# Two convolutions as four diagonal products each, and the second layer's set-up inside the mixers' plan

## The chip, the cores and the metric

The kernel runs on one core of a Trainium2 chip. The core has five engines that run side by side and wait for one another by semaphores: PE (TensorE, matrix products into PSUM), DVE (VectorE), ACT (ScalarE), POOL (GpSimd) and SP (SyncE, which here only issues DMA transfers). The metric is the device time of one execution in microseconds; before the change it is 6781.04 us, the median of three runs (6777.89 to 6788.52).

## The reference, cut to what matters

The input x has 4 images of 256 channels and 64x64 places, so 4 sequences of 4096 tokens. Two layers follow each other, and after them a mixture of experts. Everything is float32.

```python
# layer 0: a Mamba mixer with 512 inner channels and 16 states
xm, zm = split(t @ m_in_w.T)                       # 512 channels each
xp = pad(xm, 3 zeros in front of each sequence)
xc = sum(xp[:, k:k+L] * m_conv_w[:, k] for k in range(4)) + m_conv_b
xm = silu(xc)                                      # then dt, B, C from xm; a scan over the tokens:
h = exp(dt*A) * h + (dt*xm) * B ; y = (h * C).sum(states)

# layer 1: rmsnorm, one projection W_in, the same kind of convolution over 4 tokens on 512 + 128 channels
z, xBC, dt = split(rmsnorm(t, norm_w) @ W_in.T)
xBC = silu(sum(pad(xBC)[:, k:k+L] * conv_w[:, k] for k in range(4)) + conv_b)
# ... a scan with 8 heads, rmsnorm with gnorm_w, W_out; then 8 experts, each token to the best one (gate_w)
```

Each convolution multiplies a channel's last four tokens by that channel's own four weights ("taps") and adds them; no channel mixes with another.

## The kernel before

The program has three phases: `mixers` (both layers and the routing), `experts` and `turn` (back to channels first). The change is in `mixers` alone and in the host's layout of two weight arrays.

**Tiling.** Tokens are cut into 64 chunks of T = 256 (16 per sequence). A tile has 128 channels as partitions, and tokens or groups beside them. For each chunk the stages are `front0` (projection and convolution of layer 0), `mid0` (step sizes), `scan` (16 steps; each makes `ub` and `h` on DVE over 128x1024 elements, and `p` on POOL), `tail0` (output projection), `front1` (layer 1's norm, projection and convolution), `ssd` (layer 1's scan in matrix form, two chunks later) and `back1` (routing).

**Order of the work.** Before the chunks a set-up part is written out in program order (lines 442 to 614): it loads the weights, folds norm weights into them and makes small helper matrices. Loads of layer 0's weights are issued by SP, those of layer 1's by ACT's queue. After it, everything is recorded by `Plan` (line 136) rather than issued: each operation has a slot, which is its chunk's number times 16 plus the stage's own (FRONT0 = -25, MID0 = -16, scan 0 to 15, TAIL = 18, SSD = 29, BACK = 37). `Plan.order` (line 273) then places the operations by estimated durations: whenever an engine is free, it takes the ready operation with the lowest slot. The estimates are constants in `mm`, `act`, `dve`, `gps` and `dma`. The resulting order is fixed at build time; on the chip each engine runs its list in that order and waits where an input is late. Every operation of the plan has line 371 in the profile, where it is issued, so tile names tell them apart.

**Buffers.** A tile is named by a tag with a number of buffers. `raw` (the convolution's input with three tokens of the chunk before in front, the "halo") has one buffer, which both layers use in turn; `raw4` has three. In PSUM the banks are `a` (two buffers, `front0` and `mid0`), `b` (one, `tail0` and `front1`), `c` (two, `ssd` and `back1`), `ub` (one) and `py` (one). A new tile in a tag begins when the last reader of the old one is done. The halo is written by POOL (`halo`, line 661), and the last three tokens are kept by POOL for the next chunk (`keep`, line 668).

**The convolution.** `to_taps` (line 677) writes `raw` to a DRAM buffer `raw_d`. For each of the four groups j of 128 channels `tapped` (line 683) reads it back with four DMAs into `raw4`: 32 partitions per tap, each shifted by one token, four channel groups beside one another. `convolve` (line 693) makes four products with 128x32 weights, each of which fills 32 of PSUM's partitions:

```python
for i in range(SQ):
    r.mm(pi[i * R : (i + 1) * R], weights[:, j * SQ + i], raw4[:, i], start=True, stop=True)
r.act(dst, pi, AF.Identity, bias=bias[:, j : j + 1])
```

The weights `taps_m` and `taps_x` hold 16 such 128x32 matrices each. A float32 product is recorded as two matmul instructions. The remaining 128 channels of layer 1 (B and C) are convolved in another way already: `diag_bc` holds four diagonal 128x128 matrices, and `front1` (lines 1018 and 1019) adds four products over the shifted tile `rbc`.

## Time and profile before

| what | value |
|---|---|
| median of three runs | 6781.04 us |
| the profiled execution | 6786.87 us |
| its span, first to last instruction | 6785.2 us |
| PE, DVE, ACT, POOL busy | 5984.4, 5545.7, 4859.2, 3494.2 us |
| first matmul of the plan (`a<-xin,w_cen`) | 43.58 us |
| first `ub` of a scan | 110.50 us |
| `xin` loads of chunks 7 and 58 issued at | 484.68 and 4823.53 us |
| DMA moved | 1245.58 MB |
| of it `raw<-raw_d`, 2048 transfers of 128.0 KB | 3.8 us each to landing (median) |
| `raw_d<-raw`, 128 transfers of 518.0 KB | 4.2 us each to landing (median) |

"Busy" is the time in which an engine has an instruction of its own in hand; matmuls are pipelined, so PE's busy time includes the ends of products that overlap nothing. "PEclk" is the share of full clock that TensorE was granted. In lines with `<-` the tile written stands on the left and those read on the right; a number after "idle before" is the time that the engine waited, and the arrow names what ended the wait. SPq and ACTq are the queues of SP and ACT that issue DMAs. The median lies 5.8 us under the profiled execution and 4.2 us under its span.

### The profile page before, as it was taken

To read this page: it belongs to the slowest core of one execution; us is meant where nothing else is said; L and a number is where in the kernel's file an instruction comes from. 1 tells how busy PE (TensorE), PEld (TensorE's weight loads), DVE (VectorE), ACT (ScalarE), POOL (GpSimd) and SP (SyncE) were. 2 spreads that over 40 slices of the span, in tenths; PEclk is the share of its full clock that TensorE was granted. 3 is DMA by queue.
4 is the path that set the end of the run, shared out by engine and by line. 5 is a ranking of instruction groups with operands and counts; after the bars stand their busy time and mean duration, and the time that the engine had idled before them with its cause. 6 is when DMAs were issued, how large, how long until landed. Compare 5 with 4: busy or idle time off the path is not lost. (4 is left out here: it accounts for less than half of the span.)

```text
span 6785.2 us, 114276 instructions
## 1 busy us (share of the span) xinstructions
PE 5984.4 (88%) x37672; PEld 4045.8 (60%) x37672; DVE 5545.7 (82%) x7646; ACT 4859.2 (72%) x12007; POOL 3494.2 (51%) x2632
## 2 busy tenths in 40 slices
PE   5788888888888888888888888888888877999996
PEld 3455555555555555555555555555555546888885
DVE  3889999999999999999999999999999973344333
ACT  4778888888888888888888888888888852333332
POOL 3555555555555555555555555555555552333331
PEclk7889999999999999999999999999999988999998
DMA  6976777777777777777777777777777734555556
GB/s 177 254 184 179 183 181 181 181 184 184 181 181 177 180 181 183 184 182 182 183 182 183 183 183 181 184 183 183 183 183 181 178 102 152 193 193 191 187 194 243
DMA packets 1125138, 1245.58 MB, mean 184 GB/s; under 512 B 111888, under 2 KB 1093652, under 8 KB 1115330
## 3 DMA queue, kind: packets, MB, share of 16 engines
q1 hardware_dynamic: 1083458, 1008.76, 59.1%
q0 software_dynamic: 30000, 210.98, 8.8%
q10 hardware_dynamic: 11088, 18.53, 0.7%
q8 instruction: 300, 4.92, 0.3%
q14 instruction: 292, 2.39, 0.1%
HBM read 919.92 MB, written 311.63 MB: 182 GB/s over the span
## 5 line engine op out<-in xcount | busy, mean ns | idle before, releaser
L371 POOL TENSOR_TENSOR p<-h,bc 128x1024 f32<-128x1024 f32 x1024 | 2413.3, 2357 | 1995.3 <-DVE ub L371 578.3
L371 DVE TENSOR_TENSOR_SCAN h<-da,ub 128x1024 f32<-128x1024 f32 x1024 | 2338.9, 2284 | 80.4 <-ACT da L371 4.8
L371 ACT ACTIVATE da<-dt,w_m_Alog 128x255 f32<-128x255 f32 x4096 | 1830.7, 502 | 0.5 <-issue 0.5
L371 DVE TENSOR_TENSOR ub<-u,bc 128x1024 f32<-128x1024 f32 x1024 | 1269.1, 1239 | 20.2 <-DMA u<-u_d 11.3
L371 PE MATMUL py<-p,sum 128*32 128x256 f32 x8192 | 689.6, 411 | 334.1 <-POOL p L371 326.3
L371 PE MATMUL b<-t,w_W_in 128*128 128x256 f32 x2304 | 581.5, 393 | 65.1 <-ACT raw L371 26.1
L371 PEld LDWEIGHTS py<-p,sum 128*32 128x32 f32 x8192 | 180.7, 111 | 724.6 <-POOL p L371 465.2
L371 PEld LDWEIGHTS b<-t,w_W_in 128*128 128x128 f32 x2304 | 420.8, 191 | 230.6 <-ACT raw L371 90.3
L1374 PE MATMUL ph<-xt,w 128*128 128x256 f32 x2272 | 517.8, 381 | 5.2 <-ACT hid L1376 5.0
L1385 PE MATMUL po<-w,hid 128*128 128x256 f32 x2272 | 502.0, 379 | 0.0
L371 PE MATMUL a<-t,w_m_in_w 128*128 128x256 f32 x2048 | 496.6, 391 | 4.5 <-DVE t L371 4.5
L371 ACT COPY hlast<-h 128x4 f32<-128x4 f32 x1024 | 202.6, 198 | 407.3 <-DVE h L371 402.8
L1385 PEld LDWEIGHTS po<-w,hid 128*128 128x128 f32 x2272 | 431.7, 190 | 58.7
L1374 PEld LDWEIGHTS ph<-xt,w 128*128 128x128 f32 x2272 | 427.4, 191 | 64.8 <-ACT hid L1376 7.6
L371 PEld LDWEIGHTS a<-t,w_m_in_w 128*128 128x128 f32 x2048 | 377.0, 191 | 125.8 <-issue 50.6
L1351 DVE CAST number<-rows 128x2 uint32<-128x2 f32 x71 | 12.2, 172 | 486.0 <-DMA tok_d<-fixed,number 473.6
L371 PE MATMUL c<-cum,after 128*128 128x512 f32 x512 | 331.2, 752 | 83.8 <-ACT dend L371 67.3
L1349 ACT ACTIVATE tn<-rows 128x256 f32<-128x256 f32 x142 | 82.2, 597 | 421.0 <-DMA rows<-buf_d,row_at 420.6
L1397 POOL DMA_INDIRECT tok_d<-fixed,number x142 | 145.8, 1027 | 396.3 <-DVE fixed L1395 306.1
L371 ACT ACT_TABLE_LOAD x256 | 328.4, 1283 | 4.4
L371 ACT ACTIVATE cum<-upto,da 128x128 f32<-128x128 f32 x1024 | 328.7, 395 | 0.7 <-DVE da L371 0.7
L1376 ACT ACTIVATE hid<-ph,w 128x256 f32<-128x256 f32 x426 | 187.4, 468 | 143.7 <-PE ph L1374 143.1
(237 smaller groups left out, 11289.3 us busy)
## 6 DMA issues: line engine op xcount, KB each, us to landing
raw<-raw_d SPq DMA_DIRECT2D x2048, 128.0 KB, 3.8
dt<-dt_d SPq DMA_DIRECT2D x1024, 128.0 KB, 3.2
u<-u_d SPq DMA_DIRECT2D x1024, 128.0 KB, 3.9
raw_d<-raw SPq DMA_DIRECT2D x128, 518.0 KB, 4.2
gx_d<-pre SPq DMA_DIRECT2D x64, 1024.0 KB, 4.5
bc<-bc_d SPq DMA_DIRECT2D x1024, 64.0 KB, 2.4
gx<-gx_d SPq DMA_DIRECT2D x256, 256.0 KB, 5.2
dt_d<-mid SPq DMA_DIRECT2D x64, 512.0 KB, 2.9
```

The source lines that it names most:

```text
L371: op.issued = f(*map(placed, args), **{k: placed(v) for k, v in kw.items()})
L1349: act(tn[:, j], rows[:, j, TOK:], AF.Identity, scale=rows[:, j, 1:2], bias=rows[:, j, 2:3])
L1351: nc.vector.tensor_copy(number, rows[:, :, 3])
L1374: mm(ph, w1[:, k, f * P : (f + 1) * P], xt[:, k], start=k == 0, stop=k == KC - 1)
L1376: act(hid[:, f], ph, AF.Relu, bias=b1[:, f : f + 1])
L1385: mm(po[:, j], hid[:, f, j * P : (j + 1) * P], w2[:, f], start=f == 0, stop=f == KF - 1)
L1397: nc.gpsimd.indirect_dma_start(out=tok_d, out_offset=bass.IndirectOffsetOnAxis(ap=number[:, j : j + 1], axis=0), in_=fixed[:, j], in_offse ...
```

## The change

Both convolutions read `raw` in SBUF directly. The weights become 16 diagonal 128x128 matrices for each layer (four channel groups by four taps), and each group is four accumulating products of 128x128 by 256. `to_taps`, `tapped`, `raw_d` and `raw4` are gone. The host lays the tap weights out by channel. The loads and the weight arithmetic of layer 1 leave the set-up and are recorded in the plan with slots from -22 to 0, all loads on SP. The loads of layer 0 come in another order, and `neg_a0` is computed later. TAIL is 19 instead of 18, and the plan's estimate for DVE operations of at most four elements is 0.1 us more than their elements instead of 0.14. `lasting` stops the plan's list of former readers from growing for the constants; it changes no instruction by itself.

```diff
-TAIL, SSD, BACK = 18, 29, 37
+TAIL, SSD, BACK = 19, 29, 37
...
-        op = self.note("DVE", (0.06 if n > 4 else 0.14) + n / 960, ...
+        op = self.note("DVE", (0.06 if n > 4 else 0.1) + n / 960, ...
...
         w_in = load("w_in")
         w_gate = load("w_gate")
+        m_in = load("m_in_w")
+        ln_b = load("ln_b")
+        m_cw = load("m_conv_w")
+        ln_g = load("ln_g")
         b_gate = load("b_gate")
-        ln_g = load("ln_g")
-        ln_b = load("ln_b")
-        m_in = load("m_in_w")
-        m_cw = load("m_conv_w")
...
-        act(neg_a0, neg_a0, AF.Exp)
-        ts(neg_a0, neg_a0, -1.0, None, ALU.mult)
-        s_in = wp.tile([P, KC, 2 * DI + 2 * N2 + NH + NE], F32, name="w_W_in", tag="w_W_in")
-        nc.scalar.dma_start(s_in[:, :, :-NE], a["W_in"])
-        s_cw = load("conv_w", nc.scalar)
-        s_cb = load("conv_b", nc.scalar)
...
-        act(neg_a1, neg_a1, AF.Exp)
-        ts(neg_a1, neg_a1, -1.0, None, ALU.mult)
-        for k in range(KC):
-            ts(s_in[:, k, :-NE], s_in[:, k, :-NE], s_nw[:, k : k + 1], None, ALU.mult)
-        for k in range(KD):
-            ts(s_out[:, k, :C], s_out[:, k, :C], s_gn[:, k : k + 1], None, ALU.mult)
...
-        diag_d1 = diagonal(s_d, "diag_d1")
-        diag_bc = diagonal(s_cwbc, "diag_bc")
-        taps_m = taps(m_cw, "taps_m")
-        taps_x = taps(s_cw, "taps_x")
+        taps_m = diagonal(m_cw, "taps_m")
...
-        g_cen = g_w
...
-        nc.scalar.copy(s_in[:, :, -NE:], g_cen)
-        for k in range(KD):
-            pt_s = bank_a()
-            for m in range(KC):
-                nc.tensor.transpose(pt_s[:, m * P : (m + 1) * P], s_out[:, k, m * P : (m + 1) * P], ident)
...
+        act(neg_a0, neg_a0, AF.Exp)
+        ts(neg_a0, neg_a0, -1.0, None, ALU.mult)
         py = py_p.tile([P, 512], F32, name="py0", tag="py", bufs=1)
-        mm(py, ident, s_in[:, 0, :512], start=True, stop=True)
+        mm(py, ident, m_in[:, 0, :512], start=True, stop=True)
...
+        def later(n, name, shape=None):
+            r.slot(n)
+            src = a[name]
+            t = r.fixed(wp.tile(list(shape or src.shape), F32, name=f"w_{name}", tag=f"w_{name}"))
+            r.dma("SP", t if shape is None else t[:, :, : src.shape[-1]], src)
+            return t
+
+        def later_diagonal(n, scales, name):
+            k = scales.shape[1]
+            t = r.fixed(wp.tile([P, k, P], F32, name=name, tag=name))
+            for i in range(k):
+                r.slot(n + 0.2 * i)
+                r.gps("tensor_scalar", t[:, i], ident, scales[:, i : i + 1], None, ALU.mult)
+            return t
+
+        s_in = later(-22, "W_in", [P, KC, 2 * DI + 2 * N2 + NH + NE])
+        s_nw = later(-22, "norm_w")
+        s_out = later(-18, "W_out", [P, KD, C + NE])
+        s_gn = later(-18, "gnorm_w")
+        g_w = later(-18, "gate_w")
+        s_cw = later(-17, "conv_w")
+        s_cwbc = later(-17, "conv_w_bc")
+        s_d = later(-17, "Dp")
+        s_cb, s_cbbc, s_dtb, neg_a1, g_b = (
+            later(-16, n) for n in ("conv_b", "conv_b_bc", "dt_bias", "A_log", "gate_b")
+        )
+        taps_x = later_diagonal(-6, s_cw, "taps_x")
+        diag_bc = later_diagonal(-2, s_cwbc, "diag_bc")
+        diag_d1 = later_diagonal(0, s_d, "diag_d1")
+        r.slot(-8)
+        r.act(neg_a1, neg_a1, AF.Exp)
+        r.dve("tensor_scalar", neg_a1, neg_a1, -1.0, None, ALU.mult)
+        for k in range(KC):
+            r.dve("tensor_scalar", s_in[:, k, :-NE], s_in[:, k, :-NE], s_nw[:, k : k + 1], None, ALU.mult)
+        for k in range(KD):
+            r.dve("tensor_scalar", s_out[:, k, :C], s_out[:, k, :C], s_gn[:, k : k + 1], None, ALU.mult)
+        pt_s = bank_c(NE)
+        for k in range(KC):
+            r.mm(pt_s, mean_c, g_w[:, k], start=k == 0, stop=k == KC - 1)
+        for k in range(KC):
+            r.tt(g_w[:, k], g_w[:, k], pt_s, ALU.subtract)
+        r.copy(s_in[:, :, -NE:], g_w)
+        for k in range(KD):
+            pt_s = bank_c(KC, P)
+            for m in range(KC):
+                r.transpose(pt_s[:, m], s_out[:, k, m * P : (m + 1) * P], ident)
+            turned = work([P, KC, P], "sq")
+            r.copy(turned, pt_s)
+            pt_s = bank_c(NE)
+            for m in range(KC):
+                r.mm(pt_s, turned[:, m], g_w[:, m], start=m == 0, stop=m == KC - 1)
+            r.copy(s_out[:, k, C:], pt_s)
+        for t in (s_in, s_out, s_cb, s_cbbc, s_dtb, neg_a1, g_b, taps_x, diag_bc, diag_d1):
+            t.root.lasting = True
...
-        def to_taps(raw, tag):
-            d = scratch([NG, R, TAPS - 1 + T], tag)
-            r.dma("SP", spread_rows(d), raw)
-            return d
-        def tapped(d, j):
-            t = work([P, SQ, T], "raw4", 3)
-            for k in range(TAPS):
-                r.dma("SP", t[k * R : (k + 1) * R], d[j * SQ : (j + 1) * SQ, :, k : k + T].rearrange("g c l -> c g l"))
-            return t
-        def convolve(raw4, weights, j, dst, bias, get):
+        def convolve(raw, weights, j, dst, bias, get):
             pi = get(T)
-            for i in range(SQ):
-                r.mm(pi[i * R : (i + 1) * R], weights[:, j * SQ + i], raw4[:, i], start=True, stop=True)
+            for k in range(TAPS):
+                r.mm(pi, weights[:, j * TAPS + k], raw[:, j, k : k + T], start=k == 0, stop=k == TAPS - 1)
             r.act(dst, pi, AF.Identity, bias=bias[:, j : j + 1])
...
             for j in range(KD):
                 k_.at(FRONT0 + 5 + j)
-                part = tapped(d, j)
                 k_.at(FRONT0 + 7 + j)
-                convolve(part, taps_m, j, pre0[:, KC + KD + j], m_cb, bank_a)
+                convolve(raw, taps_m, j, pre0[:, KC + KD + j], m_cb, bank_a)
...
-                convolve(part, taps_x, j, pre1[:, KD + j], s_cb, bank_b)
+                convolve(raw, taps_x, j, pre1[:, KD + j], s_cb, bank_b)
...
-        return np.asarray(w).reshape(NG, R, TAPS).transpose(2, 1, 0).reshape(P, NG)
+        return np.asarray(w).reshape(KD, P, TAPS).transpose(1, 0, 2).reshape(P, KD * TAPS)
```

## The prediction

> **What bounds the kernel now.** I read the page's totals and slices first, then busy time by stage, then the waits of DVE and PE in the repeating stretch, then single groups of PE's timeline. The page's totals and slices:
>
> ```profile
> span 6785.2 us, 114276 instructions
> PE 5984.4 (88%) x37672; PEld 4045.8 (60%) x37672; DVE 5545.7 (82%) x7646; ACT 4859.2 (72%) x12007; POOL 3494.2 (51%) x2632
> ...
> PE   5788888888888888888888888888888877999996
> DVE  3889999999999999999999999999999973344333
> PEclk7889999999999999999999999999999988999998
> DMA  6976777777777777777777777777777734555556
> ```
>
> From slice 4 to slice 32 DVE is at 9 tenths and PE just below it; the last fifth (experts, output) is PE's and is not touched. The windows of the filling, the crowded beginning and the repeating stretch (busy us and instructions by engine, granted clock, DMA share, GB/s):
>
> ```profile
> 44.00:110.00 66.00, 40.05 (x152) 27.27 (x150) 6.28 (x6) 25.97 (x47) 0.58 (x3) 0.74 0.49 134
> 110.00:430.00 320.00, 242.28 (x1504) 149.79 (x1504) 276.36 (x303) 237.55 (x585) 162.38 (x110) 0.83 0.93 237
> 430.00:5250.00 4820.00, 4294.03 (x28794) 2714.10 (x28788) 4497.81 (x6002) 3985.25 (x9957) 2756.24 (x1959) 0.94 0.73 182
> ```
>
> The loads of xin of chunks 7 and 58 are 4338.85 us apart: 85.08 us per chunk, so 4820 us hold 56.7 chunks. Per chunk DVE is busy 93.3%, or 79.4 us, and idle 5.7; PE is busy 89.1%, or 75.8 us, and idle 9.3. The waits in that stretch:
>
> ```profile
> DVE xdt L371 <- PE c L371: 77.1, 131, 2.6
> DVE state L371 <- PE c L371: 55.8, 48, 1.2
> DVE gm L371 <- PE c L371: 36.1, 44, 2.6
> PE py L371 <- POOL p L371: 266.1, 204, 4.4
> PE c L371 <- ACT dend L371: 64.6, 53, 1.5
> ```
>
> DVE waits for no DMA here. What it waits for is PE's ssd products, about 3 us per chunk in these three lines. PE's longest wait is for p, the end of a scan step, 4.7 us per chunk: PE runs ahead and waits for DVE's and POOL's chain. So DVE sets the pace, and PE has slack. How much is the whole question, because the change takes from it.
>
> **What the Trainium skill says.** TensorE: Matmul & The Clock Gate, Part 1: the clock has two states, full and half, set by how busy PE was in windows of some 3.4 us. The trace agrees: slices of 10 us show 1.00, and 0.50 between 70 and 80 us; from 5700 to 6300 us, where PE is busy 595.96 of 600, it is 1.00. So the mean of 0.94 means half clock 12% of the time: it costs PE up to 0.06 x 85.08 = 5.1 us per chunk, and a denser PE may win part of it back. TensorEngine Tiling (Array Packing), Overview: weights of 32 columns leave room for four products side by side, up to 4 times faster. The trace shows close to 3, below. Perfetto Trace Analysis, Identifying the Most-Contended Engine: PE's busy share is a poor measure of its headroom; hence I count PE by products at full clock.
>
> **The price of a product.** Groups of PE's timeline (start, us, tiles, records; two records are one product):
>
> ```profile
> 3007.21 0.61 PE L371 MATMUL a<-raw,taps_m 128*32 128x256 f32 x8
> 3015.93 3.62 PE L371 MATMUL b<-g,w_m_out_w 128*128 128x256 f32 x16
> 3024.88 1.89 PE L371 MATMUL a<-pre,w_m_xproj_w 128*64 128x256 f32 x8
> 3059.46 2.00 PE L371 MATMUL b<-rbc,diag_bc 128*128 128x256 f32 x8 [0.84 <-ACT pre L371]
> ```
>
> The last line is the new form already in use, four diagonal products. Alone it is busy 2.00 us; in a backlog the second eight records of 16 cost 3.62 - 1.89 = 1.73. A tap group costs 0.61 to 0.64. A convolution group so grows by 1.1 us (1.73 - 0.64) to 1.4 (2.00 - 0.64), and a chunk has eight: 8.7 to 10.9 us more PE per chunk. I take 8.7, since PE will be backlogged.
>
> **The change part by part.**
>
> *Steady pace.* PE's need at full clock is at most 75.8 - 5.1 = 70.7 us per chunk now, and 70.7 + 8.7 = 79.4 after: as much as DVE. The 85.08 us leave 14.4 us of loss now (9.3 idle, 5.1 half clock). To hold the pace, the losses must fall to 5.7. The 4.7 us of waiting for p are slack and go first; two thirds of the half clock, 3.4 us, go if the pauses that cause it close; 0.6 must come from waits for ACT (dend, raw, bcs), which other products can fill. That just suffices. DVE's own work stays 79.4.
>
> *DMA removed.* Per chunk 2 writes of 518 KB and 32 reads of 128 KB, 34 issues by SP of about 0.45 us: 15 us less of SP's queue and 5.1 MB less. Worth nothing in the steady stretch, because DVE waits for none of it; SP's own waits for free raw4 tiles stood only before transfers that were needed later.
>
> *New holds.* raw has one buffer for both layers. It was free about 4 us after the write to DRAM; now PE's last convolution product frees it. POOL's halo copy waits for that, and POOL's p products queue behind the copy. At 3000 us layer 1 held raw from about 3046 and its convolutions end at 3076.6; layer 0's input products begin at 3066.9, so they must start some 10 us later. Layer 0's convolutions at 3000 to 3014 show that the time is there: about 52 us of 85 are held. Zero, unless POOL stands for more than two scan steps (7.3 us), the three h tiles being the cover. Bank b's single buffer is held 4 x 1.1 us longer per chunk, of some 60 us in use: also zero.
>
> *Set-up.* These are rows of the timeline from the start:
>
> ```profile
> 21.75 0.57 ACT L535 COPY w_nat<-bank_a 128x512 f32<-128x512 f32 x1
> 25.95 6.83 PE L567 MATMUL bank_a<-w_ln_b,w_m_in_w 128*128 128x1 f32 x32
> 43.58 2.64 PE L371 MATMUL a<-xin,w_cen 128*128 128x256 f32 x8
> 66.33 1.08 PE L371 MATMUL a<-raw,taps_m 128*32 128x256 f32 x8 [5.73 <-DMA raw<-raw_d]
> 110.50 1.23 DVE L371 TENSOR_TENSOR ub<-u,bc 128x1024 f32<-128x1024 f32 x1 [10.43 <-DMA u<-u_d]
> ```
>
> The w_nat copy is ready at 4.8 us, but ACT stands issuing layer 1's loads until 21.6. Afterwards: copy at 4.9, the w_gate products (3.78 us) to 9.5; m_in is third among the loads, 1.5 MB at the 191 GB/s of the first 10 us, there at about 9; the 6.83 us of L567 to 16.4; the copy 0.17 and the scaling of m_in 1.45 to 18.2; the warm-up product 2.05 to 20.3. The plan's first matmul moves from 43.6 to 20.3: 23.3 us gained. The 16 diagonals of taps_m cost POOL 16 x 0.75 = 12 us, from about 10 to 22, and are wanted at about 42.
>
> *What is moved into the plan.* 13 loads, 13 x 0.47 = 6 us of SP, which is idle from 10.5 to 48, and 1.7 MB; DVE 3.4 us, ACT about 3, PE about 8 (1.0 + 2.7 + 4.1); POOL 24 diagonals, 18 us. The window 44 to 110 shows DVE busy 6.28 of 66 and POOL 0.58, so all of it fits before layer 1 first needs it. Without that cover it would cost up to those 18 us once. I take zero.
>
> *The first chunk's convolution.* raw was ready at 58.0, the last tap group's evacuation ended at 75.2. Now PE goes on after m_in's second half (60.6): 4 x 1.73 = 6.9 and an evacuation of 0.47, at 68.0: 7 us. So the first ub comes 30 us earlier, near 80.
>
> *The crowded beginning.* From 110 to 430 us DVE is busy 86.4% against 93.3% later, 22 us lost, with DMA at 0.93 of its engines and the clock at 0.83. Tap transfers are about 5 chunks x 5.1 MB = 26 of 76 MB. Bounds are 0 and 22; I take 10.
>
> *Small estimates and TAIL 19.* They only reorder; the same operations run. Bounds of half a us per chunk either way, about 28 us; I take zero.
>
> Sum against the span: -23.3 - 7 - 10 = -40, 6785 to 6745. The median is 4 us under the span: 6781 - 40 = **6741**.
>
> **The rivals.**
>
> *PE becomes the bound (slower).* PE at 79.4 has no room for its waits. For: it would have to lose only 5.7 us per chunk where it loses 14.4; PE would be at work in 93% of the time with DVE also at 93%, each waiting for the other. If only p's 4.7 and half of the clock's loss (2.5) go, 7.2 us remain: 86.6 us per chunk, 1.5 more, 56.7 x 1.5 = 86; with 10.9 in place of 8.7 it is 3.7 more, 210. A backlogged PE is nearer the low end: 1.9 gives 6741 + 108 = **6849**. It decides at 40 / 56.7 = 0.7 us more per chunk: there the start's gain is eaten. Against: the experts' stage shows PE able to run without pauses.
>
> *The pace rises.* With DMA crossings gone, products come when the plan wants them, and PE stays at full clock just when DVE waits for ssd. Half of DVE's three waits for c, 1.5 us per chunk, saves 85: **6656**. Against: more work stands ahead of ssd's products in PE's queue.
>
> *The convolution's change is hidden both ways and the start's gain is lost again* at the first chunks, where DMA and the clearing of buf_d set the pace: **6781**.
>
> **Chances.** Pace as now, 6741 (own range 6695 to 6790): 0.45, of which 0.36 faster, 0.06 same, 0.03 slower. PE the bound: 0.30, of which 0.02 same, 0.28 slower. Pace rises: 0.20, faster. Start's gain lost: 0.05, of which 0.02 faster, 0.03 same. Together faster 0.58, same 0.11, slower 0.31, where 0.2%, 13.6 us, is about what a measurement tells from no change. The range, 6640 to 6890, leaves out the faster rival's gains above 1.8 us per chunk (0.07) and the PE rival above 2.6 (0.1).
>
> **What would show it.** First matmul of the plan near 20 us and first ub near 80, or the start's part is wrong. Groups of raw with taps of 8 records at 1.7 to 2.0 us. Chunk loads 85 us apart: under 84.4 or over 85.8 decides for a rival. If PE is the bound, its waits for p vanish, its busy share passes 95%, and DVE's waits for PE c grow beyond 3 us per chunk. If the clock stays at 0.94, the half clock was not PE's pauses. If POOL's halo copies wait for PE and DVE's scans for h, raw's single buffer is the cause.

## The result, and the profile after

The changed kernel takes 6760.62 us (median of 20 executions, 6751.93 to 6772.74) against 6779.26 us for the kernel before (20 executions, 6770.1 to 6788.52). The ratio is 0.9974, with a 95% interval of 0.9967 to 0.998: 18.6 us less, where 40 less were forecast. The profiled execution took 6757.56 us, and its span is 29.3 us shorter than the one before; 10.7 us of that are the scatter of single executions, since the medians differ by 18.6.

The page's totals and slices of the changed kernel:

```profile
span 6755.9 us, 109691 instructions
PE 6377.5 (94%) x37672; PEld 4662.5 (69%) x37672; DVE 5586.1 (83%) x7646; ACT 4890.5 (72%) x12007; POOL 3512.4 (52%) x2632
...
PE   7899999999999999999999999999999988999996
...
PEclk8999999999999999999999999999999988999998
DMA  6734443443444444434444444443444314555556
```

PE has gone from 8 tenths to 9 in nearly all of the repeating part; DMA fell from 7 tenths to 4 (908.81 MB in place of 1245.58). DVE's work is 40 us more than before with the same instructions; where that comes from is shown below. The windows of the first chunks and the repeating stretch (busy us and instructions by engine, granted clock, DMA share, GB/s):

```profile
80.00:400.00 320.00, 278.64 (x1621) 189.34 (x1620) 296.88 (x328) 260.02 (x643) 188.87 (x123) 0.93 0.66 190
400.00:5200.00 4800.00, 4604.64 (x28536) 3236.29 (x28535) 4496.37 (x5956) 3975.61 (x9865) 2735.40 (x1942) 0.99 0.41 120
```

PE is busy in 95.9% of the repeating stretch (89.1% before) and DVE in 93.7% (93.3%). The clock rose from 0.94 to 0.99. In the first chunks DVE's share rose from 86.4% to 92.8% and the clock from 0.83 to 0.93.

Following the scans through the trace gives the ledger of the profiled executions. The start of a chunk's first scan step marks the chunk:

| piece | before | after | difference, us | forecast |
|---|---|---|---|---|
| first scan step of chunk 0 | 111.9 | 82.1 | -29.8 | -30 |
| from there to chunk 8 | 683.7 | 654.1 | -29.6 | -10 |
| chunks 8 to 63, us per chunk | 85.05 | 85.60 | +0.55 x 55 = +30 | 0 |
| first to last scan step of chunk 63 | 72.7 | 71.8 | -0.9 | 0 |
| last scan step to the experts' first product | 114.7 | 121.7 | +7.0 | 0 |
| the rest | 1124.2 | 1118.4 | -5.9 | 0 |

So the start came out as forecast, the first chunks gained three times as much as forecast, and the pace, forecast to stand, rose and gave all of the first chunks' gain back. The waits in the repeating stretch of the changed kernel (total us, times, longest):

```profile
DVE stats L373 <- PE b L373: 53.2, 38, 3.8
DVE gm L373 <- PE c L373: 51.6, 45, 1.5
...
DVE xdt L373 <- PE c L373: 13.5, 48, 0.3
...
PE a L373 <- ACT pre L373: 65.7, 53, 1.4
...
PE py L373 <- POOL p L373: 24.3, 38, 2.0
```

PE's wait for `p` fell from 4.7 us per chunk to 0.4, as the budget asked. DVE's waits for `xdt` and `state` (77.1 and 55.8 us before, in about the same stretch) are nearly gone, but a wait of `stats` for bank `b` and a longer one of `gm` stand in their place: DVE's idle time per chunk is 5.4 us, and was 5.6; its work is 80.2 us, and was 79.5 (both counted from chunk 8 to 63). Two convolution groups of PE's timeline in the changed kernel (start, us, tiles, records):

```profile
3027.81 1.89 PE L373 MATMUL b<-raw,taps_x 128*128 128x256 f32 x8
...
3049.16 3.62 PE L373 MATMUL a<-raw,taps_m 128*128 128x256 f32 x16
```

A convolution group is 1.89 us alone and 1.73 (3.62 - 1.89) in a backlog, the price used in the forecast.

The start, in the rows of the changed kernel that answer to those shown of before (start, us, engine, line, tiles; the last is the first `ub` of all):

```profile
9.04 3.75 PE L533 MATMUL bank_a<-w_ln_b,w_m_in_w 128*128 128x1 f32 x32
...
17.51 2.89 PE L373 MATMUL a<-xin,w_cen 128*128 128x256 f32 x8
...
76.97 1.23 DVE L373 TENSOR_TENSOR ub<-u,bc 128x1024 f32<-128x1024 f32 x1 [6.63 <-DMA u<-u_d]
```

The plan's first matmul is at 17.5, forecast 20.3 (before 43.6); the first `ub` is at 77.0, forecast near 80. The 32 small products took 3.75 us here and not 6.83, but that is not what made the start early: with the same set-up they take anything from 3.75 to 6.96 us in the experiments below, and the plan's first matmul comes between 17.5 and 19.6 in all of them. The first scan step of the changed kernel then still waited 3.9 us for ACT's `da`, so it came at 82.1.

One thing was not foreseen. Two engines late in a scan in the changed kernel (start, us, engine):

```profile
3207.54 1.23 DVE L373 TENSOR_TENSOR ub<-u,bc 128x1024 f32<-128x1024 f32 x1
...
3211.36 2.35 POOL L373 TENSOR_TENSOR p<-h,bc 128x1024 f32<-128x1024 f32 x1
3211.39 3.40 DVE L373 TENSOR_TENSOR ub<-u,bc 128x1024 f32<-128x1024 f32 x1
```

The `ub` that begins 0.03 us after a `p` takes 3.40 us in place of 1.23 and ends 1.08 us after that `p`: nearly the whole of `p`, and then about its own time. The Trainium skill (SBUF — State Buffer, Who interferes with whom) says that a DVE instruction with two inputs in SBUF contends with a GpSimd instruction that reads SBUF, that the ports that they share are an exclusive lock, and that the order of issue decides who is blocked; both read SBUF here, and the numbers agree: `p`, which came first, keeps its 2.35. From chunk 8 to 63 the mean of `ub` rose from 1238 to 1352 ns (+1.8 us per chunk), while that of `decay`, of which a chunk has two, fell from 1616 to 1215 (-0.8). In the whole run 133 `ub` overlap a `p` by more than 0.2 us after, 24 before; 38 of the 133 take over 3 us and lie between chunks 8 and 63. The planner does not mean them to overlap: in its own times such a `p` ends just as the `ub` begins, and on the chip it runs later.

### The profile page after: what moved, and what is told of

Same layout as the page of the kernel before. It is cut to its first block, busy times and chain, and to the rows that moved or that the text cites. A ratio compares the mean times of both kernels' runs of the same rounds, so it can differ in the third digit from the quotient of the medians.

```text
span 6755.9 us, 109691 instructions
## 1 busy us (share of the span) xinstructions
PE 6377.5 (94%) x37672; PEld 4662.5 (69%) x37672; DVE 5586.1 (83%) x7646; ACT 4890.5 (72%) x12007; POOL 3512.4 (52%) x2632
## 2 busy tenths in 40 slices
DMA packets 762611, 908.81 MB, mean 135 GB/s; under 512 B 77072, under 2 KB 731156, under 8 KB 752834
## 5 line engine op out<-in xcount | busy, mean ns | idle before, releaser
L373 DVE TENSOR_TENSOR_SCAN h<-da,ub 128x1024 f32<-128x1024 f32 x1024 | 2338.4, 2284 | 108.7 <-ACT hlast L373 16.4
L373 DVE TENSOR_TENSOR ub<-u,bc 128x1024 f32<-128x1024 f32 x1024 | 1375.7, 1343 | 16.8 <-DMA u<-u_d 6.6
L373 PE MATMUL py<-p,sum 128*32 128x256 f32 x8192 | 644.0, 396 | 65.5 <-POOL p L373 63.5
L373 PE MATMUL a<-raw,taps_m 128*128 128x256 f32 x2048 | 485.4, 387 | 71.3 <-ACT pre L373 71.2
L373 PE MATMUL b<-raw,taps_x 128*128 128x256 f32 x2048 | 497.2, 385 | 28.0 <-ACT pre L373 27.5
L373 PEld LDWEIGHTS a<-raw,taps_m 128*128 128x128 f32 x2048 | 376.7, 190 | 158.8 <-ACT pre L373 100.5
L373 PEld LDWEIGHTS b<-raw,taps_x 128*128 128x128 f32 x2048 | 376.4, 189 | 152.7 <-ACT pre L373 80.7
L373 PE MATMUL a<-t,w_m_in_w 128*128 128x256 f32 x2048 | 474.8, 385 | 4.4 <-DVE t L373 2.1
```

The source lines that it names most:

```text
L373: op.issued = f(*map(placed, args), **{k: placed(v) for k, v in kw.items()})
```

## The experiments

Each was measured beside the kernel before on the same chip; its ratio is given with the 95% interval, and the pace is that of chunks 8 to 63 in its profile.

### First questions: the collision, PE's sum, the two halves of the change

Theory 1 was that the pace rose because `p` stands beside `ub`. A `p` that the plan lets end just as a DVE operation begins, with DVE idle for over 1 us before it, is made to wait for that operation:

```diff
-        return sorted(self.ops, key=lambda o: (o.start, o.seq))
...
+            held = [d for d in line if abs(d.start - op.end) < 0.011 and d.port]
...
+            if d.start - last.end > 1.0 and d not in op.deps:
+                op.behind = d
+                key[op] = (d.start, d.seq + 0.5)
+        return sorted(self.ops, key=lambda o: key.get(o, (o.start, o.seq)))
```

> The changed kernel in the same order on every engine; only those p products on POOL for which the plan lets DVE stand idle more than 1 us (56 of 1024, nearly one per chunk, mostly just ahead of the ub of a scan's last step) wait for the DVE operation that follows, so that they run beside the next scan step. Theory 1, that the pace is lost because such a p runs beside that ub and stretches it from 1.23 to 3.40 us: ub's mean falls from 1343 ns to about 1240, 1.7 us less DVE work per chunk, the pace from 85.5 to about 83.8 us per chunk, the time from 6761 to about 6665 us. Rival, that PE with its added products is the bound: PE's need is unchanged, the pace stays within 0.3 us, the time within 6745 to 6775; ub shortens all the same and DVE's waits for PE take its place.

Measured: 6774.54 us, 0.9987 (0.998 to 0.9993), pace 85.90. `ub` fell to 1274 ns and DVE's work by 1.15 us per chunk, but its idle time grew by 1.45. The waits of DVE in the repeating stretch of this kernel:

```profile
DVE stats L386 <- PE b L386: 59.2, 42, 3.8
DVE cdec L386 <- DMA cc<-bcs: 54.1, 27, 3.3
```

A wait of up to 3.3 us for the transfer of `cc`, which DVE did not have before, has taken the place. The collision is real, but taking it away in this manner gave nothing. That is what the rival expected, but for the wait: it had named PE, and the new one is for a transfer. Theory 1 alone does not explain the pace. The same rule on the kernel before:

> The kernel before with the same rule: 57 p products, 54 of them just ahead of a decay product on DVE, wait for it. Theory 1: decay's mean of 1591 ns falls to about 1220, 0.75 us less per chunk, 6779 to about 6735 us; less than in the changed kernel, because the collision here is 0.4 us per decay instead of 2.2 per ub. If the rule does something else to the kernels than take away this collision, both gain the same. Rival, PE the bound only after the change: the kernel before gains here and the changed one doesn't.

Measured: 6956.13 us, 1.0254 (1.024 to 1.0268), pace 88.31. `decay` went to 1218 ns as meant, but `ub` to 1349, and DVE waited 134.4 us for `xdt`. The rule itself makes a worse order there; it says nothing for theory 1 or against it, and it shows that this removal does more than remove a collision.

Theory 2 was PE's sum. Two of each convolution's four products are not issued, in the changed kernel's own order, so the kernel leaves out half of each convolution:

```diff
                 r.mm(pi, weights[:, j * TAPS + k], raw[:, j, k : k + T], start=k == 0, stop=k == TAPS - 1)
+                if k in (1, 2):
+                    r.ops[-1].calls.pop()
```

> The changed kernel in its own planned order, with the second and third tap's products of both convolutions not issued (the output isn't the reference's): 16 products, 16 x 0.43 = 6.9 us less PE work per chunk, everything else the same. Rival, PE the bound: the pace falls from 85.5 by at least 2 us to that of DVE's work and its few waits, 83.5 or less, the time by 110 us or more. Theory 1: PE only waits more, for p; the ub collision stays, the pace stays at 84.8 to 85.6, the time within 6715 to 6765; the granted clock falls back from 0.99 towards 0.94 as PE gets pauses again.

Measured: 6744.56 us, 0.9945 (0.993 to 0.996), pace 85.26. PE was busy 5.3 us less per chunk (76.6, and 81.9 in the changed kernel) and the pace fell by 0.34, far from the 2 us of the rival. But the clock fell back too, as expected: TensorE stood at half clock for 4.8 us per chunk, and for 2.7 in the changed kernel. So the run takes work from PE and slows PE at once, and cannot say alone that PE's sum is no limit; the table at the end of this section tells the two apart. Then each half of the change by itself. The set-up inside the plan, with the convolutions by way of DRAM and TAIL and the estimate as before:

```diff
-TAIL, SSD, BACK = 19, 29, 37
+TAIL, SSD, BACK = 18, 29, 37
...
-        taps_m = diagonal(m_cw, "taps_m")
+        taps_m = taps(m_cw, "taps_m")
...
-        def convolve(raw, weights, j, dst, bias, get):
+        def to_taps(raw, tag):
...
+        def tapped(d, j):
...
+        def convolve(raw4, weights, j, dst, bias, get):
```

> The kernel before with only the second layer's set-up inside the plan and the new order of loads (old convolution through DRAM, TAIL 18, old estimate for small operations). Prediction's sum for this part: the plan's first matmul near 17 to 20 us instead of 42.7, first scan 23 us earlier, crowded beginning as before (scans of chunks 1 to 3 take 90 us each), pace near 85.1: 6779 - 23 = 6756 us. If the crowded beginning's gain too came from the set-up and not from DMA, chunks 1 to 3 fall to 74 to 85 us here as well and the time goes to about 6730.

Measured: 6756.82 us, 0.9964 (0.9951 to 0.9978), 25.7 us less where 23 were expected; first scan step at 87.0 us in place of 111.9; the next chunks as before (68.5, 88.6, 88.2, 93.0 us). The other half, the diagonal products alone with the old set-up (but for `taps_x`, whose diagonals are made in the plan), TAIL and estimate:

```diff
-            d = to_taps(raw, "raw0_d")
...
-                part = tapped(d, j)
-                convolve(part, taps_m, j, pre0[:, KC + KD + j], m_cb, bank_a)
+                convolve(raw, taps_m, j, pre0[:, KC + KD + j], m_cb, bank_a)
```

> The kernel before with only the new convolution (diagonal products from raw; set-up in its old place but for taps_x, whose diagonals are made in the plan; TAIL 18, old estimate). If the two parts add: first matmul of the plan near 43 us as before, chunks 1 to 3 at 74 to 85 us each instead of 90, some 35 us gained up to chunk 8, and a pace 0.5 us above 85.05, 28 us lost over 55 chunks: 6770 to 6785 us. If PE's added work were nothing to the pace, 6745; if TAIL and the small estimates had saved the changed kernel from worse, 6800 or more.

Measured: 6803.98 us, 1.0033 (1.002 to 1.0045), a little slower. 6770 to 6785 was expected, and 6800 or more if TAIL and the small estimates had saved the changed kernel from worse, which fits. The first scan step came at 100.8, chunks 1 and 2 took 80.8 and 81.0 us (90.3 and 89.7 before), and the pace was 85.74. So the new convolution gains about 27 us by chunk 8 (11 of them before the first scan step) and loses 0.69 us in each of 55 chunks after it.

### The traffic

Are the first chunks faster because the transfers are gone? The old bytes were put back as transfers from DRAM to DRAM that nothing waits for, 34 per chunk, in the first six chunks, then in all:

```diff
+        def old_traffic(op):
+            op.calls.append((old_write, (), {}))
+            op.calls += [(old_read, (j, q), {}) for j in range(KD) for q in range(TAPS)]
...
+            if k_.i < 6:
+                old_traffic(r.ops[-1])
```

> The changed kernel in its own planned order, with the old transfers put back beside it for chunks 0 to 5 only (per chunk 2 copies of 512 KB and 32 of 128 KB, from x to spare DRAM, that nobody reads). Theory, that the crowded beginning's 30 us came from the transfers that are gone: scans of chunks 1 to 3 go from 74, 83 and 85 us back towards 90, DMA share above 1.0 in that stretch, first scan unchanged near 82, time up by 15 to 30 us, to 6775 to 6790. Rival, that it came from PE's full clock or the earlier set-up: less than 5 us.

> The same in all 64 chunks, 5.1 MB per chunk and 34 issues on SP. The prediction's zero for DMA in the steady stretch: the pace stays within 0.3 us of 85.6, and the time is that of the run with traffic in six chunks within 15 us. Rival, that the transfers that are gone had cost the pace too: it rises by 1 us or more per chunk, above 6830 us in all.

Measured: 6895.0 us (1.0164, 1.0147 to 1.0181) and 7866.03 us (1.159, 1.1572 to 1.1608). Both overshoot by far: in the first of them the first scan step came at 113.3 us, though it was expected to stay near 82, and chunks 1 and 2 took 112 and 110 us, more than before the change. The pace of the second was 102.42. A burst of 17 issues stood on SP's queue ahead of the loads that DVE wants; between 80 and 750 us of the first of these kernels DVE waited 95.3 us for `u` in five waits, the longest 30.4. So the two say nothing of what the old bytes had cost, in the first chunks or later. A mended form puts them one by one behind SP's other loads of those chunks:

```diff
+                            r.ops[-1].calls.insert(1, (old_read, (j, q), {}))
```

> The changed kernel in its own planned order, with the old transfers' bytes put back for chunks 0 to 5, this time one 128 KB copy before SP's queue goes on after each load of dt or u, and two of 512 KB after z (copies from x to spare DRAM, that nobody reads). Theory, that the crowded beginning was DMA's share: chunks 1 to 3 go from 74, 83, 85 us towards 90 each, 15 to 30 us in all, 6775 to 6790. If they stay below 80, 86 and 86, the share isn't the cause and the place of the transfers in SP's queue was; above 100 each, the copies cost more than the old transfers did, and the run says nothing on the size.

Measured: 6872.28 us, 1.0135 (1.0118 to 1.0153), the first scan step at 98.8 and chunks 1 to 3 at 103.1, 104.5 and 108.7 us: still above what the kernel before took, and by its own expectation this says nothing of the size. It stays open how much of the first chunks' gain is traffic and how much the shorter way from `raw` to `pre`.

### Two limits at once, the retuned numbers, the plan's patience

If two limits of about equal size stand side by side, both must be taken away. The rule for `p` and the two missing products together:

> The changed kernel in its own planned order with both: 56 p products held behind the DVE operation that follows, and two of the four taps' products not issued (the output isn't the reference's). Each alone left the pace at 85.9 and 85.3. Theory 2, two limits at nearly the same height: with the collision gone DVE is free but PE holds the pace, with PE's products gone DVE and its collision hold it; with both gone the pace falls to 84.3 or less, the time to 6690 or less. Rival, a third limit at 85 (a transfer such as cc on SP, or ACT): the pace stays at 84.8 or more and the time above 6720.

Measured: 6762.25 us, 0.9963 (0.995 to 0.9977), pace 85.78. The waits of DVE between 1000 and 5000 us there:

```profile
DVE stats L386 <- PE b L386: 58.5, 33, 4.5
DVE cdec L386 <- DMA cc<-bcs: 55.8, 28, 3.4
```

DVE and PE both had less to do, and DVE waited for bank `b` and for `cc`. Theory 2 had asked for 84.3 or less, so by the pace it fails. It is not refuted, though: TensorE was at half clock for 5.3 us per chunk here, and the eight chunks without half clock took 83.3 (table at the end of this section). What had not been touched yet is the order in which the plan puts layer 1's stages against the scan. First the two small numbers of the change, put back:

```diff
-TAIL, SSD, BACK = 19, 29, 37
+TAIL, SSD, BACK = 18, 29, 37
...
-        op = self.note("DVE", (0.06 if n > 4 else 0.1) + n / 960, ...
+        op = self.note("DVE", (0.06 if n > 4 else 0.14) + n / 960, ...
```

> The changed kernel with TAIL 18 and the estimate 0.14 as before: set-up and convolution changed, nothing else. If the parts add, it is set-up alone (6757) plus what the convolution alone costs (22): about 6779. Theory 3, that the pace is set by the order the plan happens on and not by any engine's sum: TAIL and 0.14 move the pace by half a us or more with the same work, and the time lies outside 6750 to 6772, the range of the changed kernel's runs. Rival, that the convolution's work sets it: within that range.

Measured: 6777.69 us, 1.0001 (0.9992 to 1.0011). Without them the change is worth nothing: the two halves, -25.7 and +21.7, simply add, to the 6779 expected from that. The order theory had expected a pace at least 0.5 us away from 85.60 as well, and that did not come. By its profile the first scan step comes at 79.9, the way to chunk 8 takes 670.7 us (13.0 less than before; with the two numbers 29.6 less), and the pace is 85.73. So the two numbers are worth some 19 us by the medians (25 by the two spans): 14 by chunk 8, where chunks 1, 3 and 6 take 80.8, 95.0 and 91.5 us without them and 73.7, 84.6 and 87.0 with them, and 7 by the pace. Then the plan's patience, the time that a `p` is held back for a good place:

```diff
-    PATIENCE = 4.0
+    PATIENCE = 6.0
```

> The changed kernel with the plan's patience for p, how long a p may wait for a scan step to run beside, 6 us instead of 4: the same operations in another order, in which 8 p products instead of 56 make DVE stand idle. Theory 3: pace 84.5 or less, 6700 or less, with PE's work as it is. If PE's added products were the bound, pace 85 to 86 and 6745 to 6775 whatever the order.

Measured: 6764.02 us, 0.9977 (0.9968 to 0.9986), pace 85.58, `ub` 1302 ns. DVE waited 84.7 us for `stats` and 71.1 for `hlast` between 400 and 5200 us: again less collision, the same pace, another wait. The order theory had asked for 84.5 or less here, and missed.

### The stages' slots

Layer 1's scan stage and the routing are asked for two slots (an eighth of a chunk) later:

```diff
-TAIL, SSD, BACK = 19, 29, 37
+TAIL, SSD, BACK = 19, 31, 39
```

> The changed kernel with SSD and BACK two slots later (31 and 39): the same operations in another order, with 63 p products that make DVE stand idle, 77 us in the plan against 123. Theory 3: its pace differs from 85.6 by over 0.5 us, and if the later ssd gives the transfer of cc more room, to 84.8 or less, 6715 or less. If PE were the bound: 85 to 86, 6745 to 6775.

Measured: **6640.34 us, 0.9799 (0.9783 to 0.9814)**, pace 83.50: 2% better than the kernel before and 1.8% better than the changed one, with the same instructions. The window of its repeating stretch:

```profile
400.00:5000.00 4600.00, 4458.01 (x28058) 3125.99 (x28058) 4426.77 (x5856) 3885.31 (x9704) 2653.78 (x1911) 1.00 0.41 123
```

and waits in the same stretch:

```profile
DVE gm L373 <- PE c L373: 40.2, 54, 1.0
...
DVE stats L373 <- PE b L373: 4.5, 6, 0.9
```

The wait of `stats` is gone, DVE is idle 3.2 us per chunk in place of 5.4, and PE's clock is full. `ub` takes 1389 ns (1343 in the whole run of the changed kernel): more time lost to collisions, and 2 us less per chunk. Do the two slots help because of the new convolution, or whichever way it is made? The same numbers on the kernel before, and on the kernel with the set-up alone:

```diff
-TAIL, SSD, BACK = 18, 29, 37
+TAIL, SSD, BACK = 18, 31, 39
```

> The kernel before with only SSD 31 and BACK 39 in place of 29 and 37: taps by way of DRAM, layer 1's set-up ahead of the plan. Order theory (the pace of 85 to 86 us is set by how early layer 1's scan stage is asked for, whichever way the convolutions are made): its pace falls about as much as the changed kernel's did, from 85.1 to about 83.5, and with the old start the time is about 6777 - 1.6 x 56 = 6690, ratio 0.986 to 0.989. Cost theory (the added products cost pace as soon as the order allows a shorter one): pace below 83, time under 6665. Third: the two belong together, the old way to convolve needs the early stage or has another limit (half clock, products that come late), pace 84.7 to 85.5, time within 0.4% of before.

> Layer 1's set-up inside the plan, the convolutions by way of DRAM as before, with SSD 31 and BACK 39. Order theory: pace as in the run above (about 83.5), the time 25 us below it for the earlier start, about 6665, so that it stands 25 us behind the changed kernel with the same two numbers (6640), which has the first chunks' gain of about 30 us besides. Cost theory: pace below 83 and a time under 6640, which would beat the full change. Third: pace 84.7 to 85.5, time about 6755.

Measured: 6687.22 us, 0.9843 (0.9819 to 0.9866), pace 83.67, and 6663.96 us, 0.9823 (0.9805 to 0.9842), pace 83.53. Both as the order theory had it (6690 and 6665). The window of the kernel before with the two slots:

```profile
400.00:5000.00 4600.00, 4117.64 (x27922) 2634.63 (x27920) 4317.26 (x5833) 3877.80 (x9662) 2675.66 (x1903) 0.93 0.74 185
```

PE busy 89.5% at a clock of 0.93 there, 96.9% at 1.00 with the diagonal products, and the same pace within 0.2 us. So in the eased order the change of form costs no pace in sum (TAIL and the small estimates differ too). That isn't to say that the added work is free: TensorE is at half clock for 11.4 us per chunk with the old form and for 0.7 with the new, so more work and a fuller clock come out even. What is left of the new form is the start: chunk 8's scan begins at 756.2 us with the set-up alone and at 730.0 with both, 26 us, and the times differ by 24 (by the ratios 16).

Two more values and two more removals tell how far this carries. SSD 33 with BACK 41, and SSD 30 with BACK 38:

```diff
-TAIL, SSD, BACK = 19, 29, 37
+TAIL, SSD, BACK = 19, 33, 41
```

> The changed kernel with SSD 33 and BACK 41, two slots later again. If what helped with 31 and 39 is that layer 1's scan stage no longer stands ahead of what the scan of layer 0 wants, a further shift gives little more or nothing: pace 83.0 to 84.0, time 6615 to 6670. If the pace merely differs from plan to plan without a direction, it may be anything from 83 to 86, and a pace above 84.7 would say so.

> The changed kernel with SSD 30 and BACK 38, between the values of the change (29 and 37, pace 85.6) and the eased ones (31 and 39, 83.5; with 33 and 41 it was 84.8). If the pace follows the shift smoothly: about 84.5, time 6680 to 6720. If the plans scatter: anything from 83 to 86.

Measured: 6721.89 us, 0.9907 (0.9888 to 0.9926), pace 84.84; and 6693.18 us, 0.9866 (0.985 to 0.9883), pace 84.46. So 29, 30, 31, 33 give 85.60, 84.46, 83.50, 84.84: a valley with its best value of these at 31. By its own expectation 33 spoke for scatter; with 30 in between, the four look like a valley, which four points make likely and do not prove. The two missing products and the rule for `p`, each in the eased order:

> The changed kernel with SSD 31 and BACK 39, and the products of taps 1 and 2 of both convolutions left out (the output is not the reference's), the plan the same. PE has some 6.9 us less per chunk. Order theory: 83.5 is again DVE's and the order's number, and the pace falls by less than 0.5 us, to 83.0 to 83.5 (time 6610 to 6640). Cost theory: with the order eased PE's sum is the limit (busy 97% there), and the pace falls by 1 us or more, to 82.5 or less (time under 6590).

> The changed kernel with SSD 31 and BACK 39, and those p products that the plan let end just as a DVE operation begins now wait for that DVE operation (as in the first run, there at 29 and 37). In the eased order ub takes 1389 ns on average against 1239 before: 16 x 0.15 = 2.4 us of DVE per chunk lost to p beside it. Collision theory: with the order eased this is pace, and it falls from 83.5 to 81.0 to 82.0, time 6500 to 6560. Order theory: DVE's time falls and another wait of DVE takes its place, as in the first run, pace 83.0 to 84.0, time 6610 to 6670.

Measured with the two products of each convolution left out: 6709.92 us, 0.9888 (0.987 to 0.9905), pace 84.63. Neither theory had this: with less work for PE the kernel is 70 us slower (60 by the ratios). Two groups of PE's timeline there, and after them two windows of the same stretch:

```profile
3116.20 1.49 PE L373 MATMUL c<-pre,diag_d 128*128 128x128 f32 x8 [1.77 <-DVE xdt L373]
3117.62 1.98 PE L373 MATMUL c<-decay,xdt 128*64 128x128 f32 x16
```

```profile
3114.00:3117.00 3.00, 1.23 (x12) 0.94 (x8) 3.00 (x5) 2.98 (x7) 1.23 (x1) 0.98 0.40 114
3117.00:3120.00 3.00, 3.00 (x24) 2.44 (x24) 2.39 (x2) 2.96 (x3) 1.69 (x2) 0.50 0.87 236
```

PE is busy 1.23 of 3 us and then runs at half clock, exactly under `ssd`'s products: `c<-decay,xdt` takes 1.98 us. The kernel with all four products, in the same order, fills that place with the convolution's work (24 records in 5.45 us and 8 in 1.89 ahead of `ssd`); the group of PE's timeline there that answers to the second:

```profile
3157.47 1.09 PE L373 MATMUL c<-decay,xdt 128*64 128x128 f32 x16
```

DVE's idle time in front of `pre`, which needs these products, is 1.07 us per chunk with the two products left out and 0.02 with all four: nearly all of the longer pace. The Trainium skill (TensorE: Matmul & The Clock Gate, Part 1) has the clock fall to half after an idle window of about 3.4 us. The stretch at half clock here is 3.41 us long, which agrees; the window ahead of it was not idle, so the measurement asks for less than the page does. It is no single place: in this run the chunks without half clock, the first two and the last of each image left aside, take 83.2 us on average (12 chunks), as in the kernel with all four products, and those with it 84.7 in the median (34 chunks).

The rule for `p` in the eased order: 6648.29 us, 0.9803 (0.9786 to 0.9819), pace 83.49. DVE's work fell by 1.26 us per chunk and its idle time rose by as much, nearly all of it in one wait:

```profile
DVE pre L386 <- PE c L386: 66.9, 49, 1.4
```

As the order theory had it: 83.5 again, with 1.3 us less of DVE's work in it.

The clock can be told from the order. The traces list TensorE's clock in stretches of 3.41 us or multiples of it. The table sorts the chunks from 8 on by it, again without the first two and the last of each image:

| kernel | pace, us | at half clock, us per chunk | chunks without half clock: number, mean us | chunks with one such stretch |
|---|---|---|---|---|
| before | 85.05 | 10.4 | none | none |
| changed | 85.60 | 2.7 | 18, 84.3 | 24, 86.0 |
| changed, two products left out | 85.26 | 4.8 | 1, 83.1 | 33, 84.5 |
| the same with the rule for `p` | 85.78 | 5.3 | 8, 83.3 | 21, 84.8 |
| eased | 83.50 | 0.7 | 41, 83.2 | 4, 84.8 |
| eased, two products left out | 84.63 | 4.4 | 12, 83.2 | 15, 84.7 |

Along each row, one stretch at half clock goes with 1.5 to 1.7 us more. So of the 2.1 us that the two slots gave, about half is half clock that is gone and about half a shorter chunk at full clock (84.3 to 83.2). And at like clock the products left out are worth some 1.5 us in the changed kernel's order (86.0 to 84.5) and nothing in the eased one (83.2 both times): there PE's work did hold the pace in part, and the falling clock hid it. No run changes the clock alone, but one chunk of the changed kernel shows the way from the clock to DVE (two windows, a group of PE, and DVE's wait for the group that follows it):

```profile
1869.55:1872.96 3.41, 3.41 (x16) 2.17 (x15) 2.78 (x4) 3.19 (x9) 0.00 (x0) 1.00 0.85 246
1872.96:1876.37 3.41, 3.41 (x15) 2.14 (x15) 3.31 (x4) 3.29 (x5) 2.15 (x1) 0.50 0.23 76
```

```profile
1873.98 2.08 PE L373 MATMUL b<-w_w_in,xtail 128*128 128x256 f32 x4
```

```profile
1878.90 0.76 DVE L373 BATCH_NORM_STATS2 stats<-b 128x6 f32<-128x256 f32 x2 [1.11 <-PE b L373]
```

Four chunks later, at full clock, the same group takes 1.13 us and `stats` does not wait. Of the 38 waits of `stats` in the changed kernel, 27 come within 8 us of such a fall.

What sets the pace at full clock, 84.3 in one order and 83.2 in the other, was not settled. Followed back through the trace from 5000 to 1000 us, the chain of work is PE's to 61% and DVE's to 17% in the eased changed kernel, but 39% and 26% in the eased kernel before, which has the same pace: two different chains of nearly one length. At SSD 29 the chain is PE's to 61% in the changed kernel and to 39% in the kernel before. A second buffer for `raw`, which would have taken its hold away, was not tried.

## Why the prediction was right or wrong

**The set-up and the first convolution: right.** -23.3 and -7 were forecast, together the first scan step 30 us earlier; it came 29.8 us earlier. The set-up alone measured -25.7. Part of the match is luck: the first `ub` was 33.5 us earlier, and the first scan step lost 3.9 of it again in a wait for ACT's `da` that no term had.

**The crowded beginning: right in size once its parts are told apart, open in its cause.** -10 was forecast and -29.6 is in the ledger, but without the two retuned numbers it is -13.0. The cause named, the transfers, was not shown: DMA's share did fall, from 1.01 to 0.71 in chunk 0 and from 1.03 to 0.84 in chunk 1, but putting bytes back did more harm than taking them away had done good.

**"Small estimates and TAIL 19. They only reorder; the same operations run": wrong.** Taken as zero, they are worth some 19 us, within the bounds of 28 that stood beside the zero. That the same operations run was true, and it was the wrong thing to look at.

**"Steady pace ... That just suffices": the step that failed.** It was taken as zero and measured +0.55 us per chunk, 30 us. Its working was good as far as it went: a group costs 1.73 us in a backlog, the wait for `p` went from 4.7 to 0.4, the time at half clock from 10.4 us per chunk to 2.7. One size was off: by the eased order, where PE runs at full clock, PE's need is at most 4458.01 / 4600 x 83.5 = 80.9 us per chunk, so the new form added about 10 us to the 70.7 and not the 8.7 taken, inside the 8.7 to 10.9 of the prediction. PE's losses fell to 85.6 - 80.9 = 4.7 us, below the 5.7 allowed, which did not make up for it. The step then said that a PE with just enough room holds the pace and that DVE's own work stays 79.4. The first doesn't follow, because a loss is not worth the same everywhere. The half clock that is left costs PE about 1.4 us per chunk, less than the 1.7 that the sum had let stand, but it falls on products that DVE waits for, and a chunk with one such stretch takes 86.0 us where one without takes 84.3, less than the 85.05 of before. The second was wrong too: DVE's work is 80.2, since `ub` cost 1.8 us more and `decay` 0.8 less by what the order puts beside them. Yet neither is the whole cause, for taking DVE's part away gave nothing, and what sets the 84.3 is open. The new form costs 0.4 to 0.7 us per chunk between kernels with the old TAIL and SSD at 29, and nothing in sum with SSD at 31. A sum over engines says what an order could reach, not what this order does.

**The rivals.** "PE becomes the bound" named three signs. Two came: `p`'s wait all but vanished and PE's share passed 95%. The third went the other way: DVE's three listed waits for bank `c` fell from 3.0 to 1.2 us per chunk, and it was `stats` and bank `b` that grew. The loads of `xin` of chunks 7 and 58 are 85.53 us per chunk apart, short of the 85.8 that was to decide. Its size was wrong (1.9 forecast, 0.55 measured). Its cause was in part right: the chain of work is PE's to 61% and was to 39%, and at like clock the products left out shorten the chunk by some 1.5 us. In the eased order, where they shorten it by nothing, PE's sum is not the bound although PE's share is higher still. "The pace rises" was right that full clock would take away DVE's waits for `xdt` and `state`; others took their place. "The start's gain lost again" did not come: the first chunks gained. DMA removed and new holds at zero: no wait for either shows among DVE's long ones in the changed kernel. Half of the sign for `raw`'s single buffer came, POOL's halo copy waiting 69.4 us for PE in 38 waits, but DVE's scans wait for ACT and for no such copy.

The half clock went as forecast, but not for the reason given, the pauses: see the count in the last section.

The forecast's direction held, because the start's gain was larger than the loss of pace. Of its 40 us, 18.6 are there. By profiled spans the kernel without the retuned numbers has -32 by the set-up and the first convolution, -13 in the first chunks, +37 by pace and +3 after it, together -5; the retuned numbers bring another -25, which makes the -29.3 of the two spans. By the medians the two steps are 0 and some -19.

## What to carry to other kernels

When the order of work is written down by a planner, a change that moves work from one engine to another should be judged with the stages' offsets swept again: here the change as made gave 0.3%, and moving two stages by two slots gave 1.8% more, with no instruction changed, and gave 1.6% to the kernel before. A removal that only moves the idle time to another wait, as here for `p` beside `ub`, points to a chain and not to an engine's sum. But look at the clock first: where work is taken from TensorE, compare stretches of like clock, since less work can drop the clock just ahead of the products that the others wait for, and hide what was gained or cost more than that.

## What the runs showed of the hardware

- A DVE operation over 128x1024 elements with both inputs in SBUF that began 0.03 us behind a POOL product of the same size took 3.40 us in place of 1.23, while the POOL product kept its 2.35.
- TensorE with 1.23 us of work in a stretch of 3 us ran at half clock in the next 3 us: a group of 16 records took 1.98 us that took 1.09 at full clock. But in the changed kernel the clock also fell after 3.41 us in which PE was busy throughout (the windows at 1869.55 and 1872.96 us).
- What foretells the fall is how much of the array the products use. Count the columns of every record in the 3.41 us ahead, each times the share of the 128x128 array that its weights fill; that window of the changed kernel then has 1012, and the one of the kernel with two products left out 1091. In all 20 traces between 400 and 5300 us, 1250 of 1295 falls to half clock follow a window with less than 1500, and only 130 of 24246 windows after which the clock stayed full had less. PE's busy share does not tell: 452 of the falls follow a window in which it was over 90% busy. An old tap group (eight records of 256 columns, weights of 32 columns) counts 512 and a new one 2048, which fits the clock's rise from 0.94 to 0.99 with the diagonal products. It is a count from these traces, in float32, and no run was made to try it.
- With bursts of 17 transfers on SP's queue that nothing waits for, DVE waited up to 30.4 us for a later load; the same bytes spread over the queue still made chunks 1 to 3 13 to 16 us longer than in the kernel before. In the repeating stretch of the eased order DMA's share of 0.74 with the old convolution and 0.41 with the new went with paces less than 0.2 us apart.
